# Second layer of a two-layer block: the addition of the gate's second half to x is placed behind the second pair's gate sum

## The chip, the cores and the metric

The kernel runs on one core of a Trainium2 chip, as one launch. The metric is device time in microseconds (us). "The profile" is one profiled execution, "the trace" is its record instruction by instruction. Times with a decimal point such as 235.44 are start times in us from the beginning of the profiled span.

The engines are called TensorE (PE in the profile; its weight loads are PEld), VectorE (DVE), ScalarE (ACT), GpSimd (POOL) and SyncE (SP, which issues most of the transfers).

## The reference

x is 4 batches of 512 rows of 256 columns. Two layers follow each other, both of the form x = x + s · silu(ffn(xn)), with xn the layernorm of x:

```
xn = layernorm(x)
s  = attention_or_mixer(xn)                  # layer 0: a mixer; layer 1: causal softmax attention
h  = silu(xn @ W1.T) * (xn @ W3.T)           # 1024 hidden columns
g  = silu(fwht(h) @ W2.T)                    # fwht: Walsh-Hadamard transform, folded into W2
x  = x + s * g                               # "gate": the product with s, and the addition to x
```

In the second layer s is layernorm, q/k/v products, causal scores, softmax, product with v, output projection and residual. All is float32; the kernel splits each operand into a high and a low part and adds three products.

## The kernel before, in words

All of x stays on chip, as four tiles `xs[b]` of 128 rows by 4 blocks by 256 columns. Layer 0 runs batch by batch, then layer 1 runs batch by batch (the loop `for b in range(B)` at the end, L1066). The change has an effect in layer 1 alone.

In layer 1 the gated network of batch b is `ffn_s` (L557). It takes the hidden columns in four pairs, q = 0 to 3. W1 and W3 are multiplied with a Strassen-like scheme of seven block products, which TensorE computes in a fixed order within a pair; each product is six matmuls of 256 columns (L616). The results stand in PSUM banks `gate_`, `lin` and `z`, and VectorE and ScalarE combine them between the products. In pair q, in this order:

- A11·B11 into `gate_`; copied to `lin` (L630);
- S1·T1 into `z`; copied to `h1` (L636);
- S2·T2 into `gate_`; copied to `v` (L639);
- S4·B22 into `z`; `v = z + v` (L648);
- S3·T3 into `gate_`, which has to wait until L639 has read the bank; then `h1 = gate_ + h1` (L651), the pair's gate sum;
- A12·B21 into `lin`; SiLU of `h1` on ScalarE (L600), `h1 = h1 * v` (L655), and the split into a high part (ScalarE, L61) and a low part (VectorE, L62);
- A22·T4 into `gate_`, which has to wait until L651 has read the bank; SiLU of it, times `lin` (L669), split.

In pair 1 the copies L630, L636 and L639 are done by VectorE, in the other pairs by ScalarE (L626).

Between the products lie eight places per pair. What stands there is written by hand in the table `places` (L1079 and after): the down products `dn` of the pair before, the attention of the same batch (scores `sc`, masks L813, maxima L815, exponentials L830, transposes `pt`, products `pv`), the preparation of the next batch, and the gate of the batch before. TensorE's order is fixed to that of the program (`line["fixed"]`, L1063). On the other engines a scheduler orders the instructions by its own estimate of times, within the dependencies; `with after(ins)` adds an order: what is issued inside stands behind `ins`.

The gate of batch b − 1 is made in two halves, i = 0 and i = 1, each of two blocks of 128 rows (`gate`, L686). The SiLU on ScalarE stands in pair 0, at places 4 and 7. The rest of it, the function `add` (L696), is called in pair 1:

```python
[1, later_gates[0]], [pts[1], later_gates[1]], [2], [pv[0], pv[1], 3],
```

These are places 4 to 7 of pair 1 (L1093; the last batch has the same two entries, L1108). So half 0 is called ahead of the product S3·T3, and half 1 at place 5, after the statement L651 and ahead of A12·B21. `add` issues a product with s (L699, ordered behind the moments of the next batch's layernorm), the addition to x (L700) and the store of that half (L1037, SyncE). The addition has no order of its own, so the scheduler may place it on VectorE anywhere after its product L699.

For half 1 in batch 1 of the loop VectorE's order around it is: product L699, mask L813, maximum L815, copy L636, addition L700, maximum L815, copy L639, low part `pl` of the transposes (L62), L648, reciprocal L855, low part of the hidden half (L62), sum L651, low part `pl` of the next transposes (L62), L655.

SyncE issues, in order: the store of half 0, two small transfers for the next layernorm (L445, L447), the store of half 1, and then the two transfers of the weights of pair 3 (L350), which wait until TensorE has done with the buffer of pair 1.

Of the kernel before, what the change touches and what calls it, by code (L numbers as in the profile page):

```python
# [17 lines left out]
ALU = mybir.AluOpType  # L18
# [17 lines left out]
def kernel(ctx: ExitStack, tc: tile.TileContext, a: dict, out: bass.AP):  # L36
    nc = tc.nc
# [9 lines left out]
    def t2(name, shape, dt=F32):  # L47
        return act.tile(shape, dt, tag="t2", name=name, bufs=6)
# [10 lines left out]
    def split(src, hi, lo, engine=nc.vector):  # L59

        h = nc.scalar.copy(hi, src)  # L61
        return h, engine.tensor_tensor(lo, src, hi.bitcast(F32), ALU.subtract)  # L62
# [11 lines left out]
    def matmul(*args, **kwargs):  # L74
        return in_line(nc.tensor.matmul, *args, **kwargs)
# [141 lines left out]
    def sl(i):  # L217
        return slice(i * P, (i + 1) * P)
# [240 lines left out]
    def after(ins):  # L459
        return tc.issue_after(ins.ins) if ins else nullcontext()  # L460
# [96 lines left out]
    def ffn_s(name, b, pairs, w2, beside, before, last=None):  # L557
# [16 lines left out]
        def down(q, c, hs, tiles):  # L574
            for t in tiles:
                hh, hl = (h[:, c, sl(t % 2)] for h in hs[t // 2])
                o = out_of(t)
                for n, (l, r) in enumerate(((hh, w2h), (hh, w2l), (hl, w2h))):
                    matmul(
                        o, l, r[:, 2 * q + c, :],  # L580
                        start=q + c + n == 0 and (t % 2 == 0 or last is not None),
                        stop=q == NH // 2 - 1 and c == 1 and n == 2,
                        skip_group_check=True,
                    )

        def units(q, hs):

            return [
                lambda c=c, tiles=tiles: down(q, c, hs, tiles) for tiles in ((0, 1), (2, 3)) for c in range(2)
            ]  # L590

        def bank(n):
            return psum(f"{name}gu{n}", [P, 2, D], tag="gu", bufs=3)

        def halves(n, dt=F32):
            return hid(f"{name}{n}", dt).rearrange("p (c n) -> p c n", c=2)

        def silu(o, i):
            with after(first["table"]):
                first["table"] = nc.scalar.activation(o, i, AF.Silu)  # L600

        hidden, behind, left = {}, before, []
        for q in range(NH // 2):
            wh, wl = pairs(q)
            places = beside[q]

            def place(n):
                for what in places[n]:
                    if isinstance(what, tuple):
                        down(what[0], what[1], hidden[what[0]], what[2])  # L610
                    elif isinstance(what, int):
                        behind[what]()
                    else:
                        what()

            def product(o, i, j, begin=False, end=False):  # L616


                for n, (w, x) in enumerate([(wh, xh), (wl, xh), (wh, xl)]):
                    for c in range(2):  # L620
                        matmul(
                            o[:, c, :], w[:, i, sl(c)], x[j],
                            start=begin and n + c == 0, stop=end and n == 2, skip_group_check=True,
                        )

            copy = nc.vector.tensor_copy if q == 1 else nc.scalar.copy  # L626
            gate_ = bank(f"{q}g")
            product(gate_, A11, B11, begin=True)
            lin = bank(f"{q}l")
            copy(lin, gate_)  # L630
            place(0)
            place(1)
            z = bank(f"{q}z")
            product(z, S1, T1, begin=True)
            h1, v, h0 = halves(f"h1_{q}"), halves(f"v{q}"), halves(f"h0_{q}")
            copy(h1, z)  # L636
            place(2)
            product(gate_, S2, T2)
            copied = copy(v, gate_)  # L639
            for what in left:  # L640
                with after(copied), after(first["table"]):
                    what()
            left = []
            place(3)
            product(z, S4, B22, end=True)

            with after(first.pop("scaled", None)):
                nc.vector.tensor_tensor(v, z, v, ALU.add)  # L648
            place(4)
            product(gate_, S3, T3)  # L650
            nc.vector.tensor_tensor(h1, gate_, h1, ALU.add)  # L651
            place(5)
            product(lin, A12, B21, end=True)
            silu(h1, h1)
            nc.vector.tensor_tensor(h1, h1, v, ALU.mult)  # L655
            hs = [(halves(f"hh{i}_{q}", F32R), halves(f"hl{i}_{q}", F32R)) for i in range(2)]
            split(h1, *hs[0])
            place(6)
            product(gate_, A22, T4, end=True)
            hidden[q] = hs  # L660
            if last is not None and q == NH // 2 - 1:

                for c in range(2):
                    silu(h0[:, c, :], gate_[:, c, :])
                    nc.vector.tensor_tensor(h0[:, c, :], h0[:, c, :], lin[:, c, :], ALU.mult)
                    split(h0[:, c, :], *(z[:, c, :] for z in hs[1]))
                break
            silu(h0, gate_)
            first["gate"] = nc.vector.tensor_tensor(h0, h0, lin, ALU.mult)  # L669

            left.append(run(split, h0, *hs[1]))
            if q:
                left.pop()()
            place(7)
            behind = units(q, hs)
# [10 lines left out]
    def gate(name, dn, s, x, store=None, halves=range(2)):  # L686

        rest = []
        for i in halves:
            ts_ = slice(2 * i, 2 * i + 2)  # L690
            g = t2(f"{name}g{i}", [P, 2, D])
            with after(first["table"]):
                first["table"] = nc.scalar.activation(g, dn[i], AF.Silu)
            rest.append((g, ts_))

        def add():  # L696
            for i, (g, ts_) in zip(halves, rest):
                with after(first.get("moments")):
                    nc.vector.tensor_tensor(g, g, s[:, ts_, :], ALU.mult)  # L699
                nc.vector.tensor_tensor(x[:, ts_, :], x[:, ts_, :], g, ALU.add)  # L700
                if store is not None:
                    store(i, ts_)

        return add
# [197 lines left out]
    def run(f, *args):  # L902
        return lambda: f(*args)
# [34 lines left out]
    first = {"table": None}  # L938
# [96 lines left out]
    def store(b):  # L1035
        def one(i, ts_):
            nc.sync.dma_start(  # L1037
                out[b, i * 2 * P : (i + 1) * 2 * P, :].rearrange("(t p) d -> p t d", p=P),
                xs[b][:, ts_, :],
            )  # L1040

        return one
# [11 lines left out]
    def pairs(b):  # L1054
        def one(q):
            for n in range(4 * b + q, min(4 * b + q + 2, 16)):
                if n not in loaded:
                    loaded[n] = load_s(n % 4, n)
            return loaded[4 * b + q]

        return one
# [4 lines left out]
    for b in range(B):  # L1066
# [15 lines left out]
        if not final:  # L1082
# [18 lines left out]
            if b + 2 < B:  # L1101
                norms[b + 2] = norm(1, b + 2)
                places[3][7].append(run(next, norms[b + 2]))
            behind, dn = ffn_s(f"f1_{b}", b, pairs(b), w2_1, places, behind)
        else:
            later = [[(q, c, (2, 3)) for c in range(2)] for q in range(2)]
# [3 lines left out]
                [[later[1][0]], [later[1][1]], [], [0], [], [1], [], []],  # L1110
            ]
            ffn_s(f"f1_{b}", b, pairs(b), w2_1, places, behind, last=gate_tile)


# [66 lines left out]
```

## Time and profile before

| what | us |
|---|---|
| median of 3 runs | 363.11 |
| lowest and highest of them | 362.93, 363.39 |
| the profiled execution | 362.72 |
| its span | 360.9 |
| around the span | 1.8 |

Two things help to read the views. A matmul's record is longer than its turn: of matmuls of 256 columns without a wait, one starts 0.12 after the other while a record has 0.28. And a group of six such matmuls of one product stands as one line with "x6"; without a wait the next one starts 0.71 after it. In the lines of the timeline the columns are start, duration, engine, line of the kernel, operation, what is written and read, and in square brackets the idle time of the engine before it with what ended it. In the lines of the waits: who waited, for whom, us in total, how often, the longest.

The names in the lines are those of the program without their numbers: `f_1gu1g` is `gate_` of batch 1, pair 1; `f_1gu1z` is `z`, `f_1gu1l` is `lin`; `f_1h` is `h1` or `h0`, `f_1v` is `v`, `f_1hh` and `f_1hl` are high and low part of the hidden columns; `g_0g` is the gate of batch 0, which is finished during batch 1; `pt` and `pl` are the transposed softmax and its low part.

### The profile page before, as it was taken

What the parts mean: (1) busy time and instruction counts of PE and PEld (TensorE: products, weight loads), DVE (VectorE), ACT (ScalarE), POOL (GpSimd) and SP (SyncE); (2) the same over time, 40 slices, a digit from 0 to 9 for tenths busy, and PEclk for the clock granted to TensorE, in tenths of its full rate; (3) what the DMA queues carried; (4) which work ended last, traced back from release to release, by engine and by line L of the source; (5) the groups of instructions that cost most, each with busy time, mean ns of one, the idle gap of its engine ahead of it and who ended that gap; (6) DMA issues with size and microseconds to landing.
All of it is one profiled execution on the core that took longest, in us unless ns stands there. A gap on an engine that the chain in (4) does not pass through costs nothing.

```text
span 360.9 us, 6262 instructions
## 1 busy us (share of the span) xinstructions
PE 354.3 (98%) x2469; PEld 327.9 (91%) x2469; DVE 286.1 (79%) x592; ACT 197.5 (55%) x372; POOL 19.0 (5%) x22
## 2 busy tenths in 40 slices
PE   8999999999999999999999999999999999999995
PEld 6878999888988898888999999999999999999995
DVE  6897868996679938898987957989679888568646
ACT  4665436274454335465467655576555676446443
POOL 1000201100011000100100001100011000000000
PEclk9999999999999999999999999999999999999999
DMA  7935000301063217637257135661554635345401
GB/s 228 346 108 186 3 0 2 116 0 60 0 196 155 118 52 236 237 130 254 85 206 261 49 157 205 223 226 79 203 205 152 215 162 203 136 149 193 194 2 58
DMA packets 16284, 52.25 MB, mean 145 GB/s; under 512 B 1632, under 2 KB 7936, under 8 KB 16256
## 3 DMA queue, kind: packets, MB, share of 16 engines
q1 hardware_dynamic: 15968, 51.60, 39.8%
q8 instruction: 19, 0.31, 0.3%
q10 hardware_dynamic: 288, 0.26, 0.2%
q14 instruction: 9, 0.07, 0.1%
HBM read 42.40 MB, written 9.45 MB: 144 GB/s over the span
## 4 chain that ended last, share of the span: by engine, by line
PE 78%; DVE 16%; ACT 2%; DMA 1%; issue 1%; POOL 1%; DVEq 0%; SPq 0%; ACTq 0%
PE f_0gu L70 6%; PE f_1gu L70 6%; PE f_0dn L70 5%; PE f_2dn L70 5%; PE f_3dn L70 5%; PE f_1dn L70 5%; PE f_3gu L70 5%; PE pv L70 4%; PE f_2gu L70 3%; PE tq L70 2%; PE o L70 2%; PE v L70 2%; PE sc L70 2%; PE warm L70 2%; DMA sraw<-in_w 1%; DVE sp L62 1%
## 5 line engine op out<-in xcount | busy, mean ns | idle before, releaser
L70 PE MATMUL f_3gu<-xt,w 128*128 128x512 f32 x96 | 25.6, 397 | 0.0
L70 PE MATMUL f_0gu<-xt,w 128*128 128x512 f32 (+1 forms) x108 | 24.9, 382 | 0.0
L70 PE MATMUL f_1gu<-xt,w 128*128 128x512 f32 x96 | 24.8, 395 | 0.0
L70 PE MATMUL f_2gu<-xt,w 128*128 128x512 f32 x96 | 24.6, 395 | 0.0
L70 PEld LDWEIGHTS f_0gu<-xt,w 128*128 128x128 f32 x108 | 18.6, 188 | 4.4 <-issue 1.0
L70 PEld LDWEIGHTS f_2gu<-xt,w 128*128 128x128 f32 x96 | 17.2, 188 | 3.2
L70 PEld LDWEIGHTS f_1gu<-xt,w 128*128 128x128 f32 x96 | 17.1, 188 | 3.2
L70 PEld LDWEIGHTS f_3gu<-xt,w 128*128 128x128 f32 x96 | 17.1, 188 | 2.9
L61 ACT CAST f_1hh<-f_1h 128x512 fp32r<-128x512 f32 x16 | 10.0, 623 | 16.7 <-DVE f_1h L524 13.6
L70 PE MATMUL f_1dn<-w2l,f_1hh 128*128 128x256 f32 x64 | 17.8, 282 | 0.0
L70 PE MATMUL f_2dn<-w2h,f_2hh 128*128 128x256 f32 x64 | 17.8, 283 | 0.0
L70 PE MATMUL f_1dn<-w2h,f_1hh 128*128 128x256 f32 x64 | 17.8, 281 | 0.0
L70 PE MATMUL f_2dn<-w2l,f_2hh 128*128 128x256 f32 x64 | 17.7, 283 | 0.0
L70 PE MATMUL f_3dn<-w2l,f_3hh 128*128 128x256 f32 x64 | 17.7, 282 | 0.0
L70 PE MATMUL f_3dn<-w2h,f_3hh 128*128 128x256 f32 x64 | 17.7, 281 | 0.0
L70 PE MATMUL f_3dn<-w2h,f_3hl 128*128 128x256 f32 x64 | 17.0, 283 | 0.4 <-DVE f_3hl L62 0.4
L70 PE MATMUL f_1dn<-w2h,f_1hl 128*128 128x256 f32 x64 | 17.1, 283 | 0.0
L70 PE MATMUL f_2dn<-w2h,f_2hl 128*128 128x256 f32 x64 | 16.8, 283 | 0.2 <-DVE f_2hl L62 0.2
L61 ACT CAST f_2hh<-f_2h 128x512 fp32r<-128x512 f32 x16 | 9.9, 621 | 12.4 <-DVE f_2h L524 9.1
L61 ACT CAST f_3hh<-f_3h 128x512 fp32r<-128x512 f32 (+1 forms) x17 | 10.1, 596 | 11.3 <-DVE f_3h L524 7.1
L62 DVE TENSOR_TENSOR f_2hl<-f_2h,f_2hh 128x512 fp32r<-128x512 f32 x16 | 10.9, 682 | 3.9 <-ACT f_2hh L61 3.8
L70 PE MATMUL f_0dn<-w2h,f_0hl 128*128 128x256 f32 x48 | 13.7, 284 | 0.1
(480 smaller groups left out, 1139.4 us busy)
## 6 DMA issues: line engine op xcount, KB each, us to landing
sw<-s SPq DMA_DIRECT2D x32, 896.0 KB, 5.5
s<-sp SPq DMA_DIRECT2D x8, 512.0 KB, 4.1
s<-sp SPq DMA_DIRECT2D x8, 384.0 KB, 2.5
w2raw<-in_w SPq DMA_DIRECT2D x4, 512.0 KB, 5.9
sraw<-in_w SPq DMA_DIRECT2D x4, 512.0 KB, 4.4
mrb<-there SPq DMA_DIRECT2D x4, 512.0 KB, 3.9
w13raw<-in_w SPq DMA_DIRECT2D x3, 512.0 KB, 6.6
x<-in_x SPq DMA_DIRECT2D x3, 512.0 KB, 3.4
```

What stands on the lines that cost most here:

```text
L61: h = nc.scalar.copy(hi, src)
L62: return h, engine.tensor_tensor(lo, src, hi.bitcast(F32), ALU.subtract)
L70: ins = call(*args, **kwargs)
```

## The change

The gate sum of each pair (L651) is remembered under the name `h1`, and the addition to x of half 1 is ordered behind the latest one. At the place where half 1 is called, that is the sum of pair 1 of the same batch. Half 0 is left as it was. In layer 0 no such sum has been issued yet, so nothing is ordered there.

```diff
@@ ffn_s @@
             product(gate_, S3, T3)
-            nc.vector.tensor_tensor(h1, gate_, h1, ALU.add)
+            first["h1"] = nc.vector.tensor_tensor(h1, gate_, h1, ALU.add)
             place(5)
@@ gate, add @@
                 with after(first.get("moments")):
                     nc.vector.tensor_tensor(g, g, s[:, ts_, :], ALU.mult)
-                nc.vector.tensor_tensor(x[:, ts_, :], x[:, ts_, :], g, ALU.add)
+                with after(first.get("h1") if i else None):
+                    nc.vector.tensor_tensor(x[:, ts_, :], x[:, ts_, :], g, ALU.add)
                 if store is not None:
                     store(i, ts_)
```

## The prediction

> **What bounds the kernel now.** I read the page first: its busy shares, then the chain that ended last.
>
> ```profile
> PE 354.3 (98%) x2469; PEld 327.9 (91%) x2469; DVE 286.1 (79%) x592; ACT 197.5 (55%) x372; POOL 19.0 (5%) x22
> ...
> PE 78%; DVE 16%; ACT 2%; DMA 1%; issue 1%; POOL 1%; DVEq 0%; SPq 0%; ACTq 0%
> ```
>
> TensorE is busy nearly throughout, but 16% of the chain runs over VectorE: there TensorE works on what it has left, and the end is set by when VectorE hands something over. So the question is where in the second layer TensorE stands still for VectorE, and whether the moved addition (L700 for the half i = 1) lies ahead of that handover. The waits of the weight loads give the places:
>
> ```profile
> PEld f_1gu1g L70 <- DVE f_1v L639: 0.3, 1, 0.3
> PEld f_2gu1g L70 <- DVE f_2v L639: 0.3, 1, 0.3
> ```
>
> Both are the product S3·T3 of pair q = 1, in batches 1 and 2. It writes the bank `gate_`, which VectorE must first have copied into v (L639). Next, the timeline of VectorE around it in batch 1 (start, duration), then that of TensorE:
>
> ```profile
> 232.38 0.67 DVE L699 TENSOR_TENSOR g_0g<-g_0g,xn 128x512 f32<-128x512 f32 x1
> ...
> 233.65 0.67 DVE L636 COPY f_1h<-f_1gu1z 128x512 f32<-128x512 f32 x1
> 234.24 0.68 DVE L700 TENSOR_TENSOR x<-x,g_0g 128x512 f32<-128x512 f32 x1
> 234.84 0.68 DVE L815 TENSOR_REDUCE neg<-sc 128x1 f32<-128x512 f32 x1
> 235.44 0.67 DVE L639 COPY f_1v<-f_1gu1g 128x512 f32<-128x512 f32 x1
> ...
> 237.77 0.68 DVE L651 TENSOR_TENSOR f_1h<-f_1gu1g,f_1h 128x512 f32<-128x512 f32 x1
> 238.37 0.54 DVE L62 TENSOR_TENSOR pl<-pt,ph 128x384 fp32r<-128x384 f32 x1
> 239.98 0.69 DVE L655 TENSOR_TENSOR f_1h<-f_1h,f_1v 128x512 f32<-128x512 f32 x1 [1.07 <-ACT f_1h L600]
> ```
>
> ```profile
> 235.78 0.28 PE L70 MATMUL f_1dn<-w2h,f_1hl 128*128 128x256 f32 x1
> 236.17 0.98 PE L70 MATMUL f_1gu1g<-tb,sw 128*128 128x256 f32 x6
> 236.99 0.49 PE L70 MATMUL pt<-ident,p 128*128 128x128 f32 x3
> ```
>
> The reader is to see three things. L700 stands two places ahead of the copy L639, with no idle time between. L639 ends at 235.44 + 0.67 = 236.11, and S3·T3 starts 0.06 later, at 236.17. And behind the place to which L700 moves (after L651) VectorE idles 1.07 us, waiting for ScalarE's SiLU.
>
> **What the Trainium skill says.** "PSUM — Partial Sum Buffer", section "Engine vs sequencer instructions": ScalarE's and VectorE's queues are strict FIFO, and matmuls start and end in program order. So L639 can't pass L700, and TensorE can't run the transposes ahead of S3·T3; the start times above agree (235.44 after 234.84 after 234.24; 236.99 after 236.17). The same page, "PSUM bank collisions raise a hardware error": accesses of two engines to one bank must be kept apart by software, so the whole product waits for the copy of the whole bank; the 0.06 us from copy to product agrees. "Perfetto Trace Analysis", section "DVE / Act Engine Instruction": a record ends with the acknowledged write, and the next instruction may begin before that. So an addition occupies less of the queue than its record shows: the starts above are 0.60 apart at 0.68 of duration, and 0.60 is what I move.
>
> **The change, part by part.** The order of instructions in the changed kernel shows L700 of half 1 moved from behind L636 to directly behind L651, in batches 1, 2 and 3; TensorE's, GpSimd's and SyncE's orders are the same. In batch 3 a few neighbours on VectorE and ScalarE change places too. Nothing is added or removed: three additions of 0.60 move.
>
> Batch 1, the removal. L815 starts at 234.24 instead of 234.84, and L639 at 234.84 (its input, the product S2·T2, began at 233.38 and lasts 0.88, so it is ready at 234.26), ending at 235.51. TensorE's last product ahead of S3·T3 starts at 235.78, and matmuls of 256 columns start 0.12 apart, so TensorE is free at 235.90. The copy is then 0.39 early: the stall goes and TensorE is next. What it costs today: from 235.90 to the transposes at 236.99 are 1.09 us, where six such matmuls without a wait take 0.71 (238.75 to 239.46 for the same shape). That is 0.38: 0.27 of standing and 0.11 of refilling. Removing the 0.60 thus gives 0.38, since TensorE is ready only 0.27 earlier.
>
> Batch 1, what is late next. ScalarE's exponential of the last scores starts at 235.56 either way (behind its predecessor), so its cast of the hidden half stays at 236.23, and the subtraction behind it (0.65 from start to start, as in batch 3: 329.74 to 330.39) starts at 236.88 instead of 237.19. L651 then starts at 237.48 and ends at 238.17. Its customer is the product A22·T4, which TensorE, now 0.38 earlier, reaches at 238.37 instead of 238.75. That holds with 0.14 to spare after the 0.06 of handover.
>
> Batch 1, the landing. L700 starts at 238.08, the subtraction for `pl` at 238.68, and VectorE is free at about 239.2. ScalarE's cast of the second transposes, its table load and SiLU all follow TensorE's transposes, so they come 0.38 earlier, and L655 can start at 239.60. Of the 1.07 us of cover, about 0.4 stays, and L700 costs nothing; without this cover it would cost up to 0.60. `pl` itself is wanted by the third PV product at 245.59.
>
> SyncE's queue. It holds the store of the half behind L700, and behind the store the next weights:
>
> ```profile
> 235.72 0.81 SPq L1037 DMA_DIRECT2D out<-x  x1
> 239.41 0.80 SPq L350 DMA_DIRECT2D sw<-s  x2
> ```
>
> The store moves to about 238.8. Issues of this store take 0.39 to 1.25, so the weights, which TensorE releases at about 239.0, go out up to 1.0 later at worst. They land 5.5 us after issue (the page's median), so by 245.6, and pair 3 wants them at 253.22: over 7 us of cover. Cost: none.
>
> Batch 2 is the same 47 us later: TensorE is free at 282.78 + 0.12 = 282.90, transposes at 283.97, so 1.07 − 0.71 = 0.36.
>
> Batch 3 differs:
>
> ```profile
> 325.40 0.29 DVE L813 TENSOR_TENSOR sc<-sc,mask 128x128 f32<-128x128 f32 x1
> 325.61 0.68 DVE L700 TENSOR_TENSOR x<-x,g_2g 128x512 f32<-128x512 f32 x1
> 326.22 0.30 DVE L813 TENSOR_TENSOR sc<-sc,mask 128x128 f32<-128x128 f32 x1
> ```
>
> Here L700 fills a gap: the next mask waits for scores that TensorE finishes at 325.78 + 0.40 = 326.18. Taking it out frees nothing before 326.22, and L639 (328.36) waits for its product anyway. What changes is the neighbours: with `pl` ahead of L651 and the subtraction ahead of L648, L651 can start when its product ends, at about 330.85 instead of 331.00. Today L651 ends at 331.69 and A22·T4 starts at 331.74, where TensorE would be free at 330.88 + 0.80 = 331.68: 0.06 of standing and 0.10 of refill, 0.16. L700 then lands in an idle stretch of 1.39 ahead of L655.
>
> Sum: 0.38 + 0.36 + 0.16 = 0.90 us. From there to the end TensorE is the chain, and its other stalls in batches 1 to 3 (the largest 0.2, for L669 ahead of the product S1·T1 of pair 2) follow events that shift with it, so the 0.90 should reach the end. The profiled execution took 362.72 (span 360.9 and 1.8 around it): 361.8. The median of the runs, 363.11, lies 0.39 above that execution, so the same gain gives 362.2.
>
> The cost with no row of its own is L700 at its new place. From above: 0.60 in each batch, if the SiLU comes so early that nothing covers it. From below: no gain of its own, since nobody waits for x but the store. I take zero.
>
> **The rivals.** (1) A second wait replaces the first: L651 is late. Its chain over the exponential, cast and subtraction on ScalarE isn't shortened by the full 0.60. If TensorE waits at A22·T4 what it no longer waits at S3·T3, the time stays at 363.1, or at 362.6 for half. For it: only 0.14 to 0.23 of margin. Against it: the gain would be gone only if L651 came over 0.5 later than worked out. (2) Slower: L700 and `pl` block L655. L655 feeds cast, subtraction and L669, for which the product S1·T1 of pair 2 already waits, so all overshoot lands on TensorE. Price: 0.60 in each of three batches, 1.80, less the gain of 0.90: 364.0. It decides from the point where SiLU ends before VectorE is free; the working leaves 0.4, so it would have to be wrong by 0.7 to lose more than is won. (3) The change does nothing, because L639 was never bound by the queue. The 0.06 handover and the gapless starts speak against it, and the changed order is plain. It gives 363.1.
>
> **How the numbers follow.** A measurement of this kernel can tell about 0.2% (0.73 us) from no change, so the forecast lies just beyond the bound. Forecast 0.75: 0.66 beyond 0.2%, 0.09 within, where a margin costs some tenths. Rivals 1 and 3 together 0.14, within. Rival 2, 0.11, slower. So faster 0.66, within 0.23, slower 0.11. Range: below, 361.6, if the 0.2 at S1·T1 goes too in two batches and the runs scatter by 0.2; above, 363.0, which takes in rival 1 for the greater part and leaves out rival 2.
>
> **What would show it.** In the changed trace: S3·T3 of pair 1 directly behind its predecessor in batches 1 and 2, and no wait on L639; L639 ahead of TensorE by some 0.4; L700 behind L651 and still idle time ahead of L655; A22·T4 without a wait. Wrong if a wait on L651 or L669 appears there, or if L655 follows `pl` with no gap.

## The result, and the profile after

| kernel | median us | runs | ratio to before, 95% interval |
|---|---|---|---|
| before | 363.10 | 12 | |
| changed | 362.31 | 12 | 0.9978 (0.997 to 0.9986) |
| changed, once more beside other kernels | 362.36 (before: 363.14) | 13 (19) | 0.9978 (0.9969 to 0.9986) |

The change takes 0.79 us off, and 0.78 in the repetition. The forecast was 0.90 us less and 362.2 us. The first interval is 0.14% to 0.30% less, or 0.51 to 1.09 us: it contains the measured and the forecast gain and excludes no change. The profiled execution of the changed kernel took 362.47, with a span of 360.7.

The page after, the same two lines as before:

```profile
PE 353.8 (98%) x2469; PEld 327.8 (91%) x2469; DVE 286.3 (79%) x592; ACT 197.2 (55%) x372; POOL 19.0 (5%) x22
...
PE 89%; DVE 6%; DMA 2%; ACT 1%; issue 1%; DVEq 0%; SPq 0%; ACTq 0%
```

Nothing was added or removed, so the busy times stay. VectorE has 6% of the chain instead of 16%: where TensorE no longer waits, the chain followed back stays on TensorE. The share isn't the price of the waits, as the prediction's reading of the 16% could suggest. 10% of the span is 36 us, and the gain is 0.8; lin_alone below takes off about 1.0 us and keeps 16%. The waits of the weight loads, after: the two lines for L639 are gone, and what is left of 0.3 and less reads

```profile
PEld f_0dn L70 <- DVE f_0hl L62: 0.3, 1, 0.3
...
PEld f_2gu2z L70 <- issue: 0.2, 1, 0.2
PEld f_1gu2z L70 <- issue: 0.2, 1, 0.2
```

The last two are the product S1·T1 of pair 2. The profile names no engine for its wait, but the product starts 0.14 to 0.15 behind the end of L669, and in lin_first below, where L669 comes earlier, the wait is gone.

VectorE in batch 1 of the changed kernel (the addition has become L701, the maximum L816):

```profile
234.17 0.68 DVE L636 COPY f_1h<-f_1gu1z 128x512 f32<-128x512 f32 x1
234.77 0.68 DVE L816 TENSOR_REDUCE neg<-sc 128x1 f32<-128x512 f32 x1
235.37 0.68 DVE L639 COPY f_1v<-f_1gu1g 128x512 f32<-128x512 f32 x1
...
238.02 0.68 DVE L651 TENSOR_TENSOR f_1h<-f_1gu1g,f_1h 128x512 f32<-128x512 f32 x1
238.62 0.68 DVE L701 TENSOR_TENSOR x<-x,g_0g 128x512 f32<-128x512 f32 x1
239.22 0.55 DVE L62 TENSOR_TENSOR pl<-pt,ph 128x384 fp32r<-128x384 f32 x1
240.13 0.69 DVE L655 TENSOR_TENSOR f_1h<-f_1h,f_1v 128x512 f32<-128x512 f32 x1 [0.36 <-ACT f_1h L600]
```

and TensorE there:

```profile
236.31 0.28 PE L70 MATMUL f_1dn<-w2h,f_1hl 128*128 128x256 f32 x1
236.43 0.88 PE L70 MATMUL f_1gu1g<-tb,sw 128*128 128x256 f32 x6
237.14 0.49 PE L70 MATMUL pt<-ident,p 128*128 128x128 f32 x3
```

The copy L639 ends at 236.05, TensorE comes free at 236.31 + 0.12 = 236.43 and starts S3·T3 at once; the transposes follow after 0.71 instead of 0.82. L701 stands where 1.07 us of idle time were, and 0.36 of it is left.

**How the gain is read.** The two spans differ by 0.2 us only, and that would mislead. The second layer of this profiled execution began late, because of a transfer of the second layer's weights during the first layer, which the change doesn't touch. It began 0.14 later and took 0.40 longer, 0.54 in all. The chain of each, first before, then after:

```profile
158.48 5.35 DMA sraw<-in_w
```

```profile
158.62 5.75 DMA sraw<-in_w
```

So I compare, matmul by matmul, when the same one starts in the two traces, and look where the difference steps:

| from TensorE's work at | before | after | difference |
|---|---|---|---|
| start of layer 2 | 172.56 | 173.10 | +0.54 |
| batch 1, transposes behind S3·T3 | 236.99 | 237.14 | +0.15 |
| batch 2, the same | 283.97 | 283.73 | −0.24 |
| batch 3, behind A22·T4 of pair 1 | 332.55 | 332.17 | −0.38 |
| batch 3, behind S1·T1 of pair 2 | 337.27 | 337.01 | −0.26 |

The steps are −0.39, −0.39, −0.14 and +0.12: 0.80 in all, which agrees with the medians. The last one is a loss that I hadn't forecast. Its lines in the trace before, first VectorE, then TensorE:

```profile
335.61 0.68 DVE L669 TENSOR_TENSOR f_3h<-f_3h,f_3gu1l 128x512 f32<-128x512 f32 x1
```

```profile
336.44 0.28 PE L70 MATMUL f_3dn<-w2h,f_3hl 128*128 128x256 f32 x1
336.55 0.89 PE L70 MATMUL f_3gu2z<-tb,sw 128*128 128x256 f32 x6
337.27 0.88 PE L70 MATMUL f_3gu2g<-tb,sw 128*128 128x256 f32 x6
```

and after:

```profile
335.39 0.68 DVE L669 TENSOR_TENSOR f_3h<-f_3h,f_3gu1l 128x512 f32<-128x512 f32 x1
```

```profile
336.06 0.28 PE L70 MATMUL f_3dn<-w2h,f_3hl 128*128 128x256 f32 x1
336.22 0.95 PE L70 MATMUL f_3gu2z<-tb,sw 128*128 128x256 f32 x6
337.01 0.88 PE L70 MATMUL f_3gu2g<-tb,sw 128*128 128x256 f32 x6
```

TensorE reaches this product 0.38 earlier than before, L669 ends only 0.22 earlier. Before, S1·T1 came 0.11 behind its predecessor, without a wait. After, it comes 0.16 behind it and then takes 0.79 instead of 0.72.

### The profile page after: what moved, and what is told of

It is laid out like the page before. It is cut to its first block, busy times and chain, and to the rows that moved or that the text cites. A ratio compares the mean times of both kernels' runs of the same rounds, so it can differ in the third digit from the quotient of the medians.

```text
span 360.7 us, 6260 instructions
## 1 busy us (share of the span) xinstructions
PE 353.8 (98%) x2469; PEld 327.8 (91%) x2469; DVE 286.3 (79%) x592; ACT 197.2 (55%) x372; POOL 19.0 (5%) x22
## 4 chain that ended last, share of the span: by engine, by line
PE 89%; DVE 6%; DMA 2%; ACT 1%; issue 1%; DVEq 0%; SPq 0%; ACTq 0%
PE f_0dn L70 6%; PE f_1dn L70 6%; PE f_0gu L70 6%; PE f_1gu L70 6%; PE f_2dn L70 5%; PE f_3dn L70 5%; PE f_3gu L70 5%; PE sc L70 4%; PE pv L70 4%; PE v L70 3%; PE f_2gu L70 3%; PE tq L70 2%; PE o L70 2%; DMA sraw<-in_w 2%; PE warm L70 2%; DVE sp L62 1%
```

## The experiments

Theory: what counts is the 0.60 us ahead of L639 in VectorE's queue; the new place is free. Rivals: the gain is the scheduler's new order in batch 3, or the place itself matters, or the addition at the new place costs something that the gain hides. All kernels keep TensorE's order. Each ratio is to the kernel before on the same chip. In the tables of starts "step" is the change of the difference to the trace before.

### Which batches carry it: b12 and b3

```diff
-                with after(first.get("h1") if i else None):
+                with after(first.get("h1") if i and name != "g1_2" else None):   # b12
+                with after(first.get("h1") if i and name == "g1_2" else None):   # b3
```

> The addition of half 1 is pinned behind the gate sum in batches 1 and 2 alone; batch 3 keeps VectorE's and ScalarE's order of before. Theory (the gain is the 0.60 us taken from ahead of the copy L639): both stalls at S3*T3 of pair 1 go, 0.38 and 0.39 less, about 362.3 us, the whole of the change's gain. Rival (the gain is the scheduler's new order in batch 3): no gain, 363.1.

> Pinned in batch 3 alone, with the new order of the neighbours there. The prediction's sum has 0.16 for it, 362.9 us. The reading of the trace after the change: 0.14 won at A22*T4 of pair 1 and 0.12 given back at S1*T1 of pair 2, which waits for L669, so 363.1. Rival (the reshuffle carries the gain): 362.3.

b12: 362.15 against 362.90, ratio 0.9981 (0.9972 to 0.9989); steps −0.36 and −0.39 at S3·T3, none in batch 3. b3: 362.72 against 362.90, ratio 0.9995 (0.9987 to 1.0003); steps −0.15 at A22·T4 and +0.11 at S1·T1 of pair 2. The two batches carry the change. Batch 3 gives nothing that these runs can tell from zero. That its small gain is handed back one product later is what the trace shows.

### Any operation there: filler

```diff
-            copied = copy(v, gate_)
+            filler = None
+            for _ in range(1 if q == 1 and b else 0):
+                with after(filler):
+                    filler = nc.vector.tensor_tensor(h1, h1, h1, ALU.max)
+            with after(filler):
+                copied = copy(v, gate_)
```

> The changed kernel with one more operation of 128x512 on VectorE between the copies L636 and L639 of pair 1 in batches 1 to 3 (h1 becomes the maximum of h1 and h1, so nothing changes in value). Theory: any 0.60 us in that stretch of the queue brings the stall back in batches 1 and 2 (0.27 and 0.11 each), none in batch 3, where L639 has time to spare: 363.1 us, as before the change. Rival (what counts is where the addition stands): 362.3.

363.09 against 362.90, ratio 1.0001 (0.9993 to 1.001). The addition is still at its new place, but the stall is back in batch 1 (the filler is L642, the copy has become L644):

```profile
234.57 0.69 DVE L642 TENSOR_TENSOR f_1h<-f_1h 128x512 f32<-128x512 f32 x1
235.17 0.69 DVE L644 COPY f_1v<-f_1gu1g 128x512 f32<-128x512 f32 x1
```

```profile
235.53 0.28 PE L70 MATMUL f_1dn<-w2h,f_1hl 128*128 128x256 f32 x1
235.91 0.99 PE L70 MATMUL f_1gu1g<-tb,sw 128*128 128x256 f32 x6
```

The product starts 0.38 behind its predecessor, 0.05 after the copy's end at 235.86, and against the trace before there is no step in batches 1 and 2. One thing was missed: in batch 3 A22·T4 lost 0.15, since the gate sum came late there and ended at 331.55, 0.06 ahead of the product's start at 331.61. That is the first rival of the prediction, in the one batch with little margin.

### The addition nearly taken out, at either place: few_new and few_old

```diff
-                nc.vector.tensor_tensor(x[:, ts_, :], x[:, ts_, :], g, ALU.add)
+                few = slice(0, 8) if i and name.startswith("g1") else slice(None)
+                nc.vector.tensor_tensor(x[:, ts_, few], x[:, ts_, few], g[:, :, few], ALU.add)
```

> The changed kernel, but the addition of half 1 covers only 8 of 256 columns (the rest of x is stored without its gate), so it occupies about 0.1 us at the new place instead of 0.60. Theory: the new place costs nothing, since 0.36 to 1.0 us of idle time are left ahead of L655: 362.3 us, the same as the changed kernel. Rival (the addition delays L655 and with it S1*T1 of pair 2): faster than the changed kernel by 0.3 us or more, 362.0 or less.

> The kernel before, but the addition of half 1 covers only 8 of 256 columns (the rest of x is stored without its gate). It stays at the old place, ahead of L815 and L639, with about 0.1 us instead of 0.60. Theory: L639 comes 0.5 earlier, the stalls go in batches 1 and 2: 362.3 us, as if it had been moved. Rival (place or order matters): 363.1.

few_new, made from the changed kernel: 362.12, ratio 0.9976 (0.9966 to 0.9986). few_old, made from the kernel before: 362.12, ratio 0.9975 (0.9966 to 0.9984). Both leave 248 of the 256 columns of half 1 without their gate, and both equal the changed kernel (0.9978). In batch 1 of few_old, first VectorE, then TensorE:

```profile
234.39 0.17 DVE L701 TENSOR_TENSOR x<-x,g_0g 128x16 f32<-128x16 f32 x1
...
235.08 0.68 DVE L639 COPY f_1v<-f_1gu1g 128x512 f32<-128x512 f32 x1
```

```profile
235.94 0.28 PE L70 MATMUL f_1dn<-w2h,f_1hl 128*128 128x256 f32 x1
236.06 0.88 PE L70 MATMUL f_1gu1g<-tb,sw 128*128 128x256 f32 x6
```

The product follows its predecessor after 0.12, without a wait. At the old place, making the addition small is worth as much as moving it; at the new place it is worth nothing that can be measured. So the move makes the addition's 0.60 us free, and the place has no effect of its own. In batches 1 and 2 few_old has VectorE's order of before. In batch 3 the scheduler gave it the changed kernel's order of the neighbours, and it has the changed kernel's steps there as well, −0.14 and +0.11: what little batch 3 shows comes with that order, whether the addition moves or not.

### How much room there is at the new place: new2 and new3

```diff
                     nc.vector.tensor_tensor(x[:, ts_, :], x[:, ts_, :], g, ALU.add)
+                for _ in range(1 if i and name.startswith("g1") else 0):     # new3: range(2 ...
+                    with after(first["h1"]):
+                        nc.vector.tensor_tensor(g, g, g, ALU.max)
```

> The changed kernel with one more 128x512 operation on VectorE behind the addition of half 1 (g becomes the maximum of g and g, nothing changes in value); the scheduler puts it behind pl and ahead of L655. Theory: L655 comes 0.24 and 0.18 later in batches 1 and 2, but behind it VectorE waits for the PV product anyway, so of that 0.1 us or less arrives at S1*T1 of pair 2: 362.4 us. Rival (the prediction's third case: overshoot lands whole on TensorE): 0.24 + 0.18 more, 362.7; with no cover at all 0.60 in each batch, 364.1.

> As new2, with two more operations; the second one stands between L655 and the two updates of xn. Theory: there no cover is left, the updates, the low part and L669 come about 0.7 later in batches 1 and 2 and 0.6 in batch 3, and S1*T1 of pair 2 waits for L669: 0.7 + 0.7 + 0.5 more than the changed kernel, 364.2 us. If the cover were larger than read from the trace: 362.4 to 363.

new2: 362.17, ratio 0.998 (0.997 to 0.999), the changed kernel's time. A second operation of this size is free too: L655 slips, but the updates of xn behind it wait for TensorE anyway. new3: 363.62, ratio 1.0017 (1.001 to 1.0024), slower than before. VectorE, then TensorE, in batch 1 of new3 (the additional operations are L704):

```profile
240.06 0.69 DVE L655 TENSOR_TENSOR f_1h<-f_1h,f_1v 128x512 f32<-128x512 f32 x1
240.66 0.68 DVE L704 TENSOR_TENSOR g_0g<-g_0g 128x512 f32<-128x512 f32 x1
...
242.65 0.68 DVE L669 TENSOR_TENSOR f_1h<-f_1h,f_1gu1l 128x512 f32<-128x512 f32 x1
```

```profile
243.48 0.95 PE L70 MATMUL f_1gu2z<-tb,sw 128*128 128x256 f32 x6 [0.56 <-DVE f_1h L669]
```

No idle time is left, and S1·T1 of pair 2 waits for L669. Steps there: +0.60, +0.54 and, in batch 3, +0.72 over the down products ahead of it and S1·T1 itself. I had expected 1.9 more than the changed kernel. It was about 1.4 by the ratios, since in batch 2 TensorE wins 0.28 back in pair 3. There it makes the transformed queries (`tq`) for the attention of the next batch, and waits for VectorE otherwise. This is the prediction's slower case, made to happen: its mechanism is real, and the point from which it costs time lies between one and two additional operations.

### The next wait: lin_first, lin_alone and both

```diff
-            split(h1, *hs[0])
+            if q == 1 and last is None:
+                nc.scalar.copy(hs[0][0], h1)
+            else:
+                split(h1, *hs[0])
...
             first["gate"] = nc.vector.tensor_tensor(h0, h0, lin, ALU.mult)
+            if q == 1 and last is None:
+                with after(first["gate"]):
+                    nc.vector.tensor_tensor(hs[0][1], h1, hs[0][0].bitcast(F32), ALU.subtract)
```

lin_first has this in the changed kernel, lin_alone in the kernel before. "both" is lin_first with the addition of half 0 ordered behind L669 of pair 1 as well, in batches 1 and 2:

```diff
-                with after(first.get("h1") if i else None):
+                with after(first.get("h1") if i else first["gate"] if name.startswith("g1") and name != "g1_2" else None):
...
-                    [1, later_gates[0]], [pts[1], later_gates[1]], [2], [pv[0], pv[1], 3],
+                    [1], [pts[1], later_gates[1]], [2], [later_gates[0], pv[0], pv[1], 3],
```

> The changed kernel, and in pair 1 of batches 0 to 2 the product with lin (L669) stands ahead of the low part of the other hidden half, which is subtracted behind it. S1*T1 of pair 2 waits for L669 today, about 0.2 us in batches 1 and 2. Theory: L669 comes 0.25 or more earlier, that stall goes: 0.3 to 0.4 less than the changed kernel, 361.9 us. Rival (ScalarE's changed order or the later low part makes a new wait at the down products): 362.3 or more.

> The kernel before with the other order of L669 and the low part in pair 1 of batches 0 to 2, and without the pin on the addition. Theory: the stalls at S3*T3 of pair 1 stay, those at S1*T1 of pair 2 and at the transformed queries go, as far as they stood before: 1.1 us less than before (what the other order took off behind the changed kernel), 361.9. Rival (the other order pays only once the addition is out of the way): 0.3 us less or nothing.

> The changed kernel with the other order of L669, and also the addition of half 0 moved, behind L669 of pair 1 in batches 1 and 2. Theory: the copies L636 and L639 of pair 1 come another 0.60 earlier on VectorE; of TensorE's waits there only the one of S4*B22 for L636 is left, 0.03 and 0.11 us and a refill of 0.1: up to 0.2 to 0.3 less than with the other order alone, 360.8 us, a ratio of about 0.994. Rival (a later addition of half 0 delays pl or the transposes' sums): no gain, 361.1.

| kernel | median us | before beside it | ratio (95%) |
|---|---|---|---|
| lin_first | 361.04 | 362.95 | 0.9947 (0.9934 to 0.9959) |
| lin_alone | 362.11 | 363.14 | 0.9972 (0.9962 to 0.9983) |
| both | 361.62 | 363.14 | 0.9959 (0.9945 to 0.9972) |

lin_first beats the changed kernel by about 1.1 us by the ratios; I had expected 0.3 to 0.4. S1·T1 of pair 2, in batch 1 of lin_first:

```profile
241.84 0.60 PE L70 MATMUL xt_2tp<-ident,xn 128*128 128x128 f32 x4
242.19 0.95 PE L70 MATMUL f_1gu2z<-tb,sw 128*128 128x256 f32 x6
```

It follows the last line of transposes after 0.35, instead of 0.54 in the changed kernel. Against the repeated changed kernel the steps at this product are −0.19 (batch 1) and −0.21 (batch 2), as expected. Another −0.23 (batch 0) and −0.28 (batch 2) come at the transformed queries of pair 3, where TensorE waits for the low part `xgl` of their input. In batch 0 ScalarE's order is the same in both kernels, so there VectorE's new order does it alone. In the repeated changed kernel VectorE idles 0.29 and 0.31 just ahead of `pl`, and from `pl` on it works without a pause up to `xgl`. In lin_first these two gaps are gone, and `pl` starts at 197.13 instead of 197.53, while TensorE is only 0.2 earlier. In batch 2 the edit also moved two copies on ScalarE forward, and the shares weren't separated. In the traces, from the start of layer 2 to the end, lin_alone takes off 0.93 and the change of this document, in its repetition, 0.77, together 1.70; lin_first measures 1.79. The two gains add, as the theory has it for waits at two different products.

"both" didn't gain on lin_first. Its trace shows what was expected at S4·B22 (steps of −0.05 and −0.11 against lin_first), but +0.18 and +0.24 at the transformed queries of batches 1 and 2. The weight loads there wait again, in lin_first and then in both:

```profile
PEld tq L70 <- DVE xgl L62: 0.4, 2, 0.2
```

```profile
PEld tq L70 <- DVE xgl L62: 1.0, 3, 0.4
```

The addition of half 0 now stands ahead of the chain that makes `xgl` on VectorE, and pushes it back. In batch 2 not all of its 0.60 arrives: lin_first has 0.20 of idle time there, and the second `xgl` starts 0.27 later (299.70 instead of 299.43). The times of the two kernels (0.9947 and 0.9959) overlap in their intervals; the waits in the traces differ plainly.

## Why the prediction was right, point by point

- **S3·T3 in batches 1 and 2.** The forecast was 0.38 and 0.36; the steps are 0.39 and 0.39, and 0.38 twice in the repetition. The mechanism is shown by filler (put 0.60 back, and the stall is back) and by few_old (make it small at the old place, and the stall is gone). The 0.06 from copy to product doesn't test the rule on PSUM banks that the prediction names beside it: S3·T3 adds to the very sums that L639 copies, so it would have to wait without that rule.
- **What L651 does next.** Worked out: start at 237.48 on the clock of before. Measured: 238.02, in a trace that runs 0.54 late by then, so the same to 0.01. A22·T4 didn't wait in batches 1 and 2; in batch 1 it had the forecast 0.14 to spare (L651 ends at 238.70, the product starts at 238.90). The subtraction ahead of L651 did wait for ScalarE, 0.21 and 0.16, as worked out, so the 0.60 couldn't have come through whole.
- **The new place.** About 0.4 of cover was forecast; 0.36, 0.42 and 1.03 are left in the three batches. That it costs nothing is shown by few_new and new2. The cover was larger than the forecast said: the updates of xn behind L655 hide part of a delay as well.
- **SyncE.** The store went out at 239.33 and the weights at 239.83, about 0.3 later than their buffer allows (they went out at 239.41 before). No wait for them followed. (Pair 3 takes the weights up at 253.06 in the trace before, not at 253.22 as the prediction has it; with 7 us of cover that changes nothing.)
- **Batch 3: the step that failed.** The sum had 0.16 for it, and said that TensorE's "other stalls in batches 1 to 3 ... follow events that shift with it, so the 0.90 should reach the end". The 0.16 was there (0.14, and 0.16 in the repetition), but of it 0.12 and 0.11 were lost at S1·T1 of pair 2. L669 doesn't hang on A22·T4 alone. It stands on VectorE behind L655, and L655 waits for a SiLU that ScalarE does behind its cast of the second transposes and a table load. Batch 3 after, ScalarE, then VectorE:

```profile
330.94 0.48 ACT L61 CAST ph<-pt 128x384 fp32r<-128x384 f32 x1 [1.89 <-PE pt L70]
331.44 1.28 ACT L600 ACT_TABLE_LOAD   x1
332.73 0.63 ACT L600 ACTIVATE f_3h<-f_3h 128x512 f32<-128x512 f32 x1
```

```profile
333.40 0.69 DVE L655 TENSOR_TENSOR f_3h<-f_3h,f_3v 128x512 f32<-128x512 f32 x1 [1.03 <-ACT f_3h L600]
```

The second transposes stand ahead of A22·T4 in TensorE's order, so this chain didn't shift with the gain there. TensorE came 0.38 earlier than before and L669 only 0.22, and the difference of 0.16 is more than the product had to spare: 0.12, from L669's end at 336.29 and 0.14 of handover to the product's start at 336.55. b3 confirms it by itself: −0.15, +0.11. Without batch 3 the forecast is 0.74; the steps of batches 1 and 2 are 0.78, and 0.76 in the repetition, which is nearly the whole measured gain of 0.79 and 0.78.
- **The rivals.** A second wait instead of the first occurred in small: in batch 3 as above, though for L669 and not for L651, and in batch 3 of filler for L651. The slower case didn't occur; new3 shows what it takes.

## What to carry to other kernels

When an operation that nobody waits for stands in a queue ahead of a handover to the engine that bounds the kernel, its worth is the wait at that handover, including the time to get going again, not its duration. Look for the stretch of its queue that idles, and count what stands between that stretch and the next handover. For every gain, ask which of the later handovers hang on events ahead of the place of the gain: those don't shift, and they take back what exceeds their margin. And when a fraction of a per cent is at stake, compare the starts of the same instruction in two traces step by step, since the spans of single executions differ by as much for reasons elsewhere.

## What the runs showed of the hardware

- A short stall of TensorE can cost more than its length. At S3·T3 the group of six matmuls behind it takes 0.81 to 0.82 us instead of 0.71 (batch 1 before: 236.17 to 236.99; batch 2: 283.16 to 283.97). The extra lies between the first two matmuls, which start 0.22 apart instead of 0.12 (236.17 and 236.39). In batch 3 after, 0.04 of waiting at S1·T1 cost 0.12. It isn't so everywhere: behind the transposes S1·T1 of pair 2 takes 0.78 with its wait (batch 1 before, 242.95 to 243.73) and 0.79 without one (lin_first, 242.19 to 242.98), so there a stall costs its length alone.
- The handover from VectorE to TensorE took 0.05 to 0.06 from the end of the record to the start of the matmul at S3·T3 and A22·T4, but 0.14 to 0.15 at S1·T1 of pair 2 (242.80 to 242.95 and 289.78 to 289.92 before, 336.07 to 336.22 after). There the traces show the wait for VectorE as a semaphore instruction of its own, of 0.05, and the weight load behind it waits for a second semaphore, which TensorE's own matmuls raise. At S3·T3 and A22·T4 the weight load waits for VectorE itself. Whether that makes the difference wasn't tried.
